# Interleaving the last products of one head group with the first products of the next

## The chip, the cores and the metric

The kernel runs on one core of one Trainium2 chip. The metric is the device time of one execution in microseconds (us). Before the change three executions took 440.07, 439.33 and 438.74 us; the median is 439.33 us.

## The reference

For each of 8 batches b there are 112 queries with 320 channels and a context of 375 tokens with 512 channels; the last 4 tokens are prompt tokens, the other 371 are text. There are 20 heads of 16 channels. What is computed, cut to its core:

```
q   = heads(x @ W_q);  k_t, v_t = heads(text @ W_k), heads(text @ W_v)
probs_t  = softmax(q @ k_t^T * scale)                  # 112 x 371 for each head
text_out = probs_t @ v_t
qsem     = probs_t @ text;  qsem /= |qsem|             # 512 channels for each head
fused    = q @ k_ip^T * scale + 0.5 * qsem @ ip_n^T    # 4 prompt tokens
ip_out   = (softmax(fused) * spatial_mask) @ v_ip
out      = (text_out + ip_out) @ W_out + b_out + x
```

Only the norm of qsem and its products with the 4 normalised prompt tokens are needed. With the Gram matrix G = text @ text^T, the squared norm is p^T G p. So the kernel multiplies the probabilities p of a head with G, the prompt products, a column of ones and the values v at once.

## The kernel before

**Groups.** The 20 heads of a batch are cut into 5 groups of 4 heads (`steps` lists all (b, g), 40 of them). A group is the unit of work around the change. Its four heads a = 0 to 3 use the four groups of 32 rows of TensorE's array; head a lies on partitions 32a to 32a+31.

**Products.** `multiplied` is the main part. The 371 text tokens are 12 blocks of 32. For block j = 0 to 11 and for each head a, one matmul takes the transposed probabilities of the block (32 rows, 112 queries) as weights and streams the block's part of a tile `u` past them: columns 32j to 392, of which the last 21 are prompt products, ones and values. G is symmetric, so only its upper part is used: block 0 streams 392 columns, block 1 360, and so on down to 72 columns for block 10 and 40 for block 11. The sums of a head gather in one PSUM bank. In the profile each float32 matmul appears as two passes, each with its own weight load (LDWEIGHTS, engine PEld), so 48 products are 96 MATMUL records.

**What follows.** ScalarE (ACT) copies the last 21 columns of each bank to `pvs` (`value_sums`, L705). VectorE (DVE) multiplies the first 371 columns with p and sums them (`reduced`, L738; a second instruction reads the accumulator). Both read the same bank, and the second reader waits for the first; `value_sums` stands first, so DVE waits for ACT. A bank is free again when both are done.

**Coming scores.** While a group is multiplied, the scores of the group two steps ahead are computed: one matmul of 375 columns for each head (`scores`, L632), the maximum on DVE (L645), the exponential on ACT (L649), a DMA from SP that spreads p over the ring `xg` (`probabilities`). A later DVE transposition makes the weights from it (`transposed`, L672).

**Pairs.** From the second group on, groups run in pairs without other TensorE work between them; there are 17 pairs, and 34 groups in them. Between the pairs stands full-array work of 7 to 11 us (projections, Gram matrices, and pieces of `finish`, here `f`, which ends a batch), written out in `behind`. One group before the first pair and the five of the last batch stand alone. The order on the engines around the change is the order of the code: TensorE, DVE, ACT, POOL and SP are scheduled by hand.

**PSUM banks.** There are 8: four of pool `ps_qd` ("qd"), two "sc" and two "mm". The first group of a pair multiplies into qd, and its coming scores use sc and mm. The second group multiplies into sc and mm, and its coming scores use qd: the scores of heads 2 and 3 stand after block 2 and take the first two qd banks of the first group, those of heads 0 and 1 stand after block 4 and take the other two. `turn` lists the banks that the work between pairs takes.

**POOL.** `placed` (L599) copies the next group's values into the last columns of `u` when the products that read the old ones are done.

Of the kernel before, what the change touches and what calls it, by code (L numbers as in the profile page):

```python
# [8 lines left out]
F32 = mybir.dt.float32  # L9
# [11 lines left out]
def kernel(  # L21
# [14 lines left out]
    nc = tc.nc  # L36
    P = 128
    B, S, C = x.shape
# [12 lines left out]
    RG = 32  # L51
# [625 lines left out]
    def multiplied(b, g, second=False):  # L677
        s = st[b]
        xT = s.pop(("xT", g))
        banks = []  # L680
        for a in range(GROUP):

            if b == B - 1 and g % 2 and g < NG - 1:
                banks.append(bank(f"ps_qd_{b}_{g}_{a}", spare=a > 1))
            elif second:
                banks.append(bank(f"ps_qd_{b}_{g}_{a}", spare=a < 2))
            else:
                banks.append(ps_qd.tile([P, 512], F32, tag="qd", name=f"ps_qd_{b}_{g}_{a}"))
        for j in range(BLK):
            c, q = j // QN, j % QN  # L690
            for a in range(GROUP):
                nc.tensor.matmul(  # L692
                    banks[a][:S, j * RG : UW],
                    xT[a * RG : (a + 1) * RG, j, :S],
                    region(b, c)[a * RG : (a + 1) * RG, q, q * RG :],
                    start=(j == 0),
                    stop=(j == BLK - 1),
                )
            yield
        s["qd", g] = banks  # L700
# [391 lines left out]
    def stretch(n, second):  # L1092

        b, g = steps[n]
        coming = steps[n + LEAD]
        late = None if second or not n else steps[n + 1]
        tags = ("mm", "sc") if b % 2 and g == NG - 1 else ("sc", "mm")
        places = {2: (2, "qd"), 4: (0, "qd")} if second else {0: (2, tags[0]), 1: (0, tags[1])}
        for j, _ in enumerate(multiplied(b, g, second)):
            if j in places:  # L1100
                a0, tag = places[j]
                for a in (a0, a0 + 1):
                    ps = pools[tag].tile([P, 512], F32, tag=tag, name=f"ps_s_{n + LEAD}_{a}")
                    scores(*coming, a, ps=ps)
                for a in (a0, a0 + 1):
                    probabilities(*coming, a)
                if late and a0 == 0:
                    transposed(*late, BLK // 2, BLK)
            if n and not second and j % QN == QN - 1:
                placed(*steps[n + 1], (j // QN,))  # L1110
# [16 lines left out]
    def behind(n):  # L1127
# [9 lines left out]
        if b % 2 == 0 and g == 0:  # L1137
# [18 lines left out]
            if n:  # L1156
                f(b - 1, 3)
# [14 lines left out]
        elif b % 2 == 0:  # L1172
            new = nb < B - 1
            turn[:] = ["qd"] * (2 + 2 * (b > 0) + (b == 0) + (not new)) + ["qd", "mm", "mm"] * new
# [34 lines left out]
        else:  # L1209
# [6 lines left out]
            f(b - 1)  # L1216
            tr(1)
            f(b - 1)
# [3 lines left out]
    for n, (b, g) in enumerate(steps[:-NG]):  # L1222
        second = n > 0 and n % 2 == 0
# [7 lines left out]
        moved(b, g)  # L1231
        if n and not second:
            if g > 1:
                turned(b + 2)
            if b % 2 and g in (0, NG - 1):
                f(b - 1 - (g == 0))
            continue
        if second and steps[n - 1] in ((b, 2), (b, 3)):
            turned(b + 2)
# [140 lines left out]
```

## Time and profile before

| what | value |
|---|---|
| median of three runs | 439.33 us |
| profiled execution, its own time | 439.46 us |
| span of its trace | 437.7 us |
| PE busy | 428.5 us, 98% |
| PEld busy (weight loads) | 330.9 us, 76% |
| DVE, ACT, POOL busy | 327.2, 185.9, 111.9 us |
| granted TensorE clock | 1.0 throughout |

PE stands for TensorE's matmuls, PEld for its weight loads, SP for the engine that issues most DMAs. A matmul record runs from its issue to a modelled end, and matmuls overlap, so a busy PE can still be late: what counts is when the next one starts. "32*112 32x360" is a weight of 32 rows and 112 columns, and 360 streamed columns.

### The profile page before, as it was taken

The page shows a single profiled execution, that of the slowest core. Times are in us where ns is not written, and L with a number is a line of the kernel's source. Part 1 is how long each engine was busy: PE and PEld are TensorE (multiplying, and loading weights), DVE is VectorE, ACT ScalarE, POOL GpSimd, SP SyncE. Part 2 cuts the span into 40 slices and gives each one's busy share as a digit, 9 for nine tenths or more (in the row PEclk, how much of TensorE's full clock was granted, in tenths as well). Part 3 has the DMA queues.
Part 4 walks back from the last instruction along what each step waited for, and adds up shares of the span by engine and source line. Part 5 has one row for each costly group of instructions (what it writes and reads, how often), then busy time and mean ns, then how long its engine had stood idle before and what let it go on. Part 6 is the DMA issues. An engine that isn't in the chain of part 4 may idle for free. (4 is left out here: it accounts for less than half of the span.)

```text
span 437.7 us, 12978 instructions
## 1 busy us (share of the span) xinstructions
PE 428.5 (98%) x5024; PEld 330.9 (76%) x5024; DVE 327.2 (75%) x687; ACT 185.9 (42%) x649; POOL 111.9 (26%) x270
## 2 busy tenths in 40 slices
PE   8999999999999999999999999999999999999986
PEld 8856776878686896878686887778776987777883
DVE  4045486877898887786798887796888897667884
ACT  2264132414543453424543363233632463336793
POOL 4302200021061242012160234002142226026440
PEclk9999999999999999999999999999999999999999
DMA  7569955577554656576654566475755426663300
GB/s 247 154 170 254 222 128 140 143 175 169 153 137 120 179 129 151 149 169 152 153 148 111 159 137 171 140 180 129 179 151 132 127 84 173 170 150 95 102 8 26
DMA packets 57931, 64.21 MB, mean 147 GB/s; under 512 B 18368, under 2 KB 52024, under 8 KB 57870
## 3 DMA queue, kind: packets, MB, share of 16 engines
q1 hardware_dynamic: 57304, 62.66, 56.6%
q8 instruction: 40, 0.66, 0.7%
q10 hardware_dynamic: 566, 0.72, 0.5%
q14 instruction: 21, 0.17, 0.1%
HBM read 18.67 MB, written 5.32 MB: 55 GB/s over the span
## 5 line engine op out<-in xcount | busy, mean ns | idle before, releaser
L692 PE MATMUL ps_qd<-u,xgT 32*112 32x168 f32 (+11 forms) x3840 | 221.3, 355 | 1.6 <-POOL u L599 1.6
L692 PEld LDWEIGHTS ps_qd<-u,xgT 32*112 32x112 f32 x3840 | 183.4, 171 | 33.3 <-issue 7.2
L672 DVE STREAM_TRANSPOSE xgT<-xg 128x768 f32<-128x768 f32 (+1 forms) x63 | 121.2, 1949 | 11.1 <-DMA xg<-p 11.1
L649 ACT ACTIVATE p<-ps_s,nmx 112x371 f32<-112x371 f32 x160 | 84.9, 592 | 93.9 <-DVE nmx L645 86.3
L738 DVE CUSTOM_DVE_ANT_0 junk<-ps_qd,p 112x371 f32<-112x371 f32 x148 | 80.2, 542 | 33.8 <-ACT pvs L705 18.2
L645 DVE TENSOR_REDUCE nmx<-ps_s 112x1 f32<-112x371 f32 x160 | 75.9, 535 | 22.3 <-PE ps_s L632 22.2
L599 POOL COPY u<-vr 128x64 f32<-128x64 f32 x120 | 26.7, 237 | 202.1 <-PE ps_qd L692 128.0
L632 PE MATMUL ps_s<-kT,qm 32*112 32x375 f32 (+1 forms) x320 | 68.3, 483 | 1.0 <-ACT shared L723 0.7
L526 PE MATMUL ps_v<-wv_sb,ctxT 128*128 128x384 f32 (+1 forms) x192 | 63.5, 477 | 0.3 <-ACT kT L499 0.3
L526 PEld LDWEIGHTS ps_v<-wv_sb,ctxT 128*128 128x128 f32 x192 | 35.4, 190 | 20.7 <-ACT kT L499 1.2
L492 PE MATMUL ps_k<-ctxT,wk_sb 128*128 128x371 f32 x136 | 45.8, 481 | 0.0
L632 PEld LDWEIGHTS ps_s<-kT,qm 32*112 32x112 f32 x320 | 35.0, 171 | 8.7 <-ACT shared L723 1.3
L454 PE MATMUL ps_g<-ctxT 128*128 128x375 f32 (+2 forms) x168 | 36.9, 376 | 0.1
L454 PEld LDWEIGHTS ps_g<-ctxT 128*128 128x128 f32 x168 | 28.2, 191 | 9.1 <-POOL ctxT L373 0.7
L492 PEld LDWEIGHTS ps_k<-ctxT,wk_sb 128*128 128x128 f32 x136 | 24.6, 190 | 13.4 <-issue 0.5
L533 ACT COPY vext<-ps_v 128x384 f32<-128x384 f32 (+1 forms) x24 | 11.2, 465 | 39.9 <-PE ps_v L526 39.9
L651 ACT COPY ipl<-ps_s 112x4 f32<-112x4 f32 x140 | 25.2, 180 | 0.0
L705 ACT COPY pvs<-ps_qd 112x21 f32<-112x21 f32 x150 | 16.4, 186 | 18.6 <-PE ps_qd L692 18.4
L336 DVE TENSOR_SCALAR qm<-ps_q,emask 128x224 f32<-128x224 f32 (+1 forms) x25 | 8.9, 394 | 19.7 <-PE ps_q L327 19.7
L499 ACT COPY kT<-ps_k 128x371 f32<-128x371 f32 x17 | 8.0, 469 | 34.6 <-PE ps_k L492 34.6
L443 ACT ACTIVATE ug<-ps_g 128x375 f32<-128x375 f32 (+2 forms) x24 | 9.0, 376 | 31.9 <-PE ps_g L454 21.0
L444 POOL TENSOR_TENSOR ug<-ug,half 128x128 f32<-128x128 f32 (+1 forms) x24 | 10.7, 447 | 39.4 <-ACT ug L443 39.4
(160 smaller groups left out, 332.4 us busy)
## 6 DMA issues: line engine op xcount, KB each, us to landing
xg<-p SPq DMA_DIRECT2D x159, 162.3 KB
u<-ug SPq DMA_DIRECT2D x128, 99.0 KB
ct<-in_ctx_dram SPq DMA_DIRECT2D x24, 176.0 KB
vr<-vd SPq DMA_DIRECT2D x32, 120.0 KB
vip<-vipd SPq DMA_DIRECT2D x6, 560.0 KB
vd<-vext SPq DMA_DIRECT2D x4, 480.0 KB
out_dram<-ob SPq DMA_DIRECT2D x8, 140.0 KB
ct<-in_ctx_dram SPq DMA_DIRECT2D x4, 256.0 KB
```

The lines of the kernel that those rows point to most:

```text
L454: nc.tensor.matmul(ps[:, : T - t0], ctxT[:, e, t0 : t0 + P], ctxT[:, e, t0:T], start=(e == 0), stop=(e == NE - 1),)
L492: nc.tensor.matmul(ps[:, :TT], wk_sb[:, e, i * P : (i + 1) * P], s["ctxT"][:, e, :TT], start=(e == 0), stop=(e == NE - 1),)
L526: nc.tensor.matmul(ps[:, :w], ctxT[:, e, c * P : (c + 1) * P], wv_sb[:, e, :w], start=(e == 0), stop=(e == NE - 1),)
L599: nc.gpsimd.tensor_copy(region(b, c)[:, :, UV - c * P :], s["vr"][:, c * QN : (c + 1) * QN, g, :])
L632: nc.tensor.matmul(ps[:S, :w], qm[a * RG : (a + 1) * RG, i, r, j * S : (j + 1) * S], s["kT"][a * RG : (a + 1) * RG, i, :w], start=True, st ...
L645: nc.vector.tensor_reduce(nmx, ps[:S, :TT], AX.X, ALU.max, negate=True)
L649: nc.scalar.activation(p, ps[:S, :TT], AF.Exp, bias=nmx)
L651: nc.scalar.copy(s["ipl"][:, groups[g][a], :], ps[:S, TT:T])
L672: nc.vector.transpose(xT[:, j : j + n].rearrange("p j (k q) -> p q j k", q=QN), xg[:, :, j * RG : (j + n) * RG].rearrange("p q (j k) -> p ...
L692: nc.tensor.matmul(banks[a][:S, j * RG : UW], xT[a * RG : (a + 1) * RG, j, :S], region(b, c)[a * RG : (a + 1) * RG, q, q * RG :], start=(j ...
L705: nc.scalar.copy(s["pvs"][:, h, :], ps[:S, TT:UW])
L738: nc.vector.tensor_tensor_reduce(out=junk, in0=ps[:S, :TT], in1=s["p", g][:, a, :], scale=1.0, scalar=0.0, op0=ALU.mult, op1=ALU.add, accu ...
```

## The change

Three things change inside a pair; its matmuls stay the same in number and size.

First, the last two blocks (72 and 40 columns) of the first group are no longer multiplied ahead of block 0 (392 columns) of the second group. Heads 2 and 3 do the second group's block 0 while heads 0 and 1 do the first group's last two blocks, and then the other way round. At the end of the second group, heads 2 and 3 do their last two blocks ahead of heads 0 and 1.

Second, the coming scores of the second group stand after blocks 4 and 7, where they stood after blocks 2 and 4.

Third, `reduced` of the first group stands ahead of its `value_sums`, so ACT now waits for DVE on each of these banks. Of the second group the order is as before.

With these the bank lists change a little: the second group's heads 2 and 3 now take the banks that heads 0 and 1 had, and in one stage the last projection takes an mm bank. Pieces of `finish` move to other places of the same stages.

TensorE, first pair of batch 1 (groups 0 and 1), where the groups meet. The tile `ps_qd_1_0_2` is the bank of batch 1, group 0, head 2; the last number is the matmul's streamed width. Before:

```order
L692 MATMUL ps_qd_1_0_0_1124<-u_1_408,xgT_1_0_1081 112x72
L692 MATMUL ps_qd_1_0_1_1125<-u_1_408,xgT_1_0_1081 112x72
L692 MATMUL ps_qd_1_0_2_1126<-u_1_408,xgT_1_0_1081 112x72
L692 MATMUL ps_qd_1_0_3_1127<-u_1_408,xgT_1_0_1081 112x72
L692 MATMUL ps_qd_1_0_0_1124<-u_1_408,xgT_1_0_1081 112x40
L692 MATMUL ps_qd_1_0_1_1125<-u_1_408,xgT_1_0_1081 112x40
L692 MATMUL ps_qd_1_0_2_1126<-u_1_408,xgT_1_0_1081 112x40
L692 MATMUL ps_qd_1_0_3_1127<-u_1_408,xgT_1_0_1081 112x40
L692 MATMUL ps_qd_1_1_0_1225<-u_1_408,xgT_1_1_1104 112x392
L692 MATMUL ps_qd_1_1_1_1226<-u_1_408,xgT_1_1_1104 112x392
L692 MATMUL ps_qd_1_1_2_1227<-u_1_408,xgT_1_1_1104 112x392
L692 MATMUL ps_qd_1_1_3_1228<-u_1_408,xgT_1_1_1104 112x392
```

The same place after:

```order
L683 MATMUL ps_qd_1_1_2_1202<-u_1_408,xgT_1_1_1104 112x392
L683 MATMUL ps_qd_1_1_3_1203<-u_1_408,xgT_1_1_1104 112x392
L683 MATMUL ps_qd_1_0_0_1124<-u_1_408,xgT_1_0_1081 112x72
L683 MATMUL ps_qd_1_0_1_1125<-u_1_408,xgT_1_0_1081 112x72
L683 MATMUL ps_qd_1_0_0_1124<-u_1_408,xgT_1_0_1081 112x40
L683 MATMUL ps_qd_1_0_1_1125<-u_1_408,xgT_1_0_1081 112x40
L683 MATMUL ps_qd_1_1_0_1200<-u_1_408,xgT_1_1_1104 112x392
L683 MATMUL ps_qd_1_1_1_1201<-u_1_408,xgT_1_1_1104 112x392
L683 MATMUL ps_qd_1_0_2_1126<-u_1_408,xgT_1_0_1081 112x72
L683 MATMUL ps_qd_1_0_3_1127<-u_1_408,xgT_1_0_1081 112x72
L683 MATMUL ps_qd_1_0_2_1126<-u_1_408,xgT_1_0_1081 112x40
L683 MATMUL ps_qd_1_0_3_1127<-u_1_408,xgT_1_0_1081 112x40
```

The twelve products are the same; two heads' long ones now stand ahead of the short ones.

TensorE, second group of the same pair, around the coming scores of heads 0 and 1 (`ps_s_8_0`, `ps_s_8_1`). Before:

```order
L692 MATMUL ps_qd_1_1_2_1227<-u_1_408,xgT_1_1_1104 112x264
L692 MATMUL ps_qd_1_1_3_1228<-u_1_408,xgT_1_1_1104 112x264
L632 MATMUL ps_s_8_0_1264<-kT_1_406,qm_1_811 112x375
L632 MATMUL ps_s_8_1_1266<-kT_1_406,qm_1_811 112x375
L692 MATMUL ps_qd_1_1_0_1225<-u_1_408,xgT_1_1_1104 112x232
```

After:

```order
L683 MATMUL ps_qd_1_1_2_1202<-u_1_408,xgT_1_1_1104 112x168
L683 MATMUL ps_qd_1_1_3_1203<-u_1_408,xgT_1_1_1104 112x168
L632 MATMUL ps_s_8_0_1276<-kT_1_406,qm_1_811 112x375
L632 MATMUL ps_s_8_1_1278<-kT_1_406,qm_1_811 112x375
L683 MATMUL ps_qd_1_1_0_1200<-u_1_408,xgT_1_1_1104 112x136
```

They moved from behind the 264-column products to behind the 168-column ones.

DVE, then ACT, the sums and value copies of the first group of that pair, with the engines that each waits for. Before:

```order
L738 ISA junk_1_0_1217,ss_1_411<-ps_qd_1_0_0_1124,p_1_0_864 112x371 [waits Activation_49]
L738 ISA ss_1_411 112x1
L738 ISA junk_1_2_1219,ss_1_411<-ps_qd_1_0_1_1125,p_1_0_864 112x371 [waits DVE_49,Activation_49]
...
L705 COPY pvs_1_412<-ps_qd_1_0_0_1124 112x21 [waits PE_49]
L705 COPY pvs_1_412<-ps_qd_1_0_1_1125 112x21 [waits PE_49]
```

After:

```order
L743 ISA junk_1_0_1221,ss_1_411<-ps_qd_1_0_0_1124,p_1_0_864 112x371 [waits PE_49]
L743 ISA ss_1_411 112x1
L743 ISA junk_1_2_1223,ss_1_411<-ps_qd_1_0_1_1125,p_1_0_864 112x371 [waits DVE_49,PE_49]
...
L710 COPY pvs_1_412<-ps_qd_1_0_0_1124 112x21 [waits DVE_49]
L710 COPY pvs_1_412<-ps_qd_1_0_1_1125 112x21 [waits DVE_49]
```

The wait has changed sides: the sums wait for TensorE alone, and each copy for its bank's sum.

The diff, cut to its core:

```diff
-    def multiplied(b, g, second=False):
+    def product(b, g, j, heads):
         s = st[b]
-        xT = s.pop(("xT", g))
...
+        xT = s["xT", g]
+        banks = s["qd", g]
+        c, q = j // QN, j % QN
+        for a in heads:
+            nc.tensor.matmul(
+                banks[a][:S, j * RG : UW],
+                xT[a * RG : (a + 1) * RG, j, :S],
+                region(b, c)[a * RG : (a + 1) * RG, q, q * RG :],
+                start=(j == 0),
+                stop=(j == BLK - 1),
+            )
...
-    def stretch(n, second):
-
-        b, g = steps[n]
-        coming = steps[n + LEAD]
-        late = None if second or not n else steps[n + 1]
+    def pair(n):
+
+        one, two = steps[n], steps[n + 1]
+        b, g = one
         tags = ("mm", "sc") if b % 2 and g == NG - 1 else ("sc", "mm")
-        places = {2: (2, "qd"), 4: (0, "qd")} if second else {0: (2, tags[0]), 1: (0, tags[1])}
...
+        ends = (BLK - 2, BLK - 1)
+
+        products_in(b, g, ("qd",) * GROUP)
+        for j in range(BLK - 2):
+            product(b, g, j, range(GROUP))
+            if j < 2:
+                heads = (HIGH, LOW)[j]
+                coming_scores(n + LEAD, heads, tags[j])
+                coming_probabilities(n + LEAD, heads)
+            if j == 1:
+                transposed(*two, BLK // 2, BLK)
+            if j % QN == QN - 1:
+                placed(*two, (j // QN,))
+        products_in(*two, (tags[1],) * 2 + (tags[0],) * 2)
+        for there, here in ((HIGH, LOW), (LOW, HIGH)):
+            product(*two, 0, there)
+            for j in ends:
+                product(b, g, j, here)
+        del st[b]["xT", g]
+        placed(*two, (NT - 1,))
+        moved(b, g)
+        if g > 1:
+            turned(b + 2)
+        if b % 2 and g in (0, NG - 1):
+            f(b - 1 - (g == 0))
+        if g in (1, 2):
+            f(b - 1, 3 - g)
+        reduced(b, g)
+        value_sums(b, g)
+
+        b, g = two
+        for j in range(1, BLK - 2):
+            product(b, g, j, range(GROUP))
+            if j == 4:
+                coming_scores(n + 1 + LEAD, HIGH, "qd")
+                coming_probabilities(n + 1 + LEAD, HIGH)
+            if j == 7:
+                coming_scores(n + 1 + LEAD, LOW, "qd")
+                coming_probabilities(n + 1 + LEAD, LOW)
+        for heads in (HIGH, LOW):
+            for j in ends:
+                product(b, g, j, heads)
...
-            turn[:] = ["qd"] * (2 + 2 * (b > 0) + (b == 0) + (not new)) + ["qd", "mm", "mm"] * new
+            turn[:] = ["qd"] * (3 + (b > 0)) + (["qd", "mm", "mm"] if new else ["mm"])
...
-        if second:
-            f1 = steps[n - 1]
-            if f1[1] == 1 or f1[1] == 2:
-                f(f1[0] - 1)
-            value_sums(*f1)
-            reduced(*f1)
-        stretch(n, second)
...
+    for n in range(0, len(steps) - NG, 2):
+        if n:
+            pair(n - 1)
+        else:
+            alone(n)
```

HIGH is heads 2 and 3, LOW heads 0 and 1; NT is 3, QN 4, BLK 12.

More of the change, by code (lines that the diff above doesn't have):

```diff
@@ L675, in transposed, with products_in, multiplied @@
             )
[L677 removed]
+    def product(b, g, j, heads):
         s = st[b]
[L679 to L698 removed]
+        xT = s["xT", g]
[9 more added lines that the diff above has]
+            )
+    def products_in(b, g, tags):
+        st[b]["qd", g] = [
+            pools[tag].tile([P, 512], F32, tag=tag, name=f"ps_qd_{b}_{g}_{a}")
+            for a, tag in enumerate(tags)
+        ]
+    def multiplied(b, g):
+        turned_round = b == B - 1 and g % 2 and g < NG - 1
+        products_in(b, g, ("mm", "mm", "sc", "sc") if turned_round else ("qd",) * GROUP)
+        for j in range(BLK):
+            product(b, g, j, range(GROUP))
             yield
[L700 removed]
+        del st[b]["xT", g]
     def value_sums(b, g, a0=0):
@@ L1090, in turned @@
             run(("c", b), lambda: transposed_context(b), pieces)
-    def stretch(n, second):
-        b, g = steps[n]
-        coming = steps[n + LEAD]
-        late = None if second or not n else steps[n + 1]
-        tags = ("mm", "sc") if b % 2 and g == NG - 1 else ("sc", "mm")
-        places = {2: (2, "qd"), 4: (0, "qd")} if second else {0: (2, tags[0]), 1: (0, tags[1])}
[L1099 to L1110, printed above, removed]
+    LOW, HIGH = (0, 1), (2, 3)
```

38 lines of the change are left out of this document (24 added, 14 removed).

## The prediction

> **What bounds the kernel now.** I read the page first: what is busy, and which lines carry it.
>
> ```profile
> span 437.7 us, 12978 instructions
> PE 428.5 (98%) x5024; PEld 330.9 (76%) x5024; DVE 327.2 (75%) x687; ACT 185.9 (42%) x649; POOL 111.9 (26%) x270
> ...
> L692 PE MATMUL ps_qd<-u,xgT 32*112 32x168 f32 (+11 forms) x3840 | 221.3, 355 | 1.6 <-POOL u L599 1.6
> ...
> L738 DVE CUSTOM_DVE_ANT_0 junk<-ps_qd,p 112x371 f32<-112x371 f32 x148 | 80.2, 542 | 33.8 <-ACT pvs L705 18.2
> ```
>
> TensorE sets the end: it is busy for 98%, and the products (L692) are half of that. DVE waited 18.2 us for ACT's value copies ahead of its sums (last row). But matmul records overlap, so a row of the array that starts its next product late leaves no idle time. So I cut the trace by stages. The 17 pairs of groups, the last batch's first group and the sum over these 18 stretches, from the view by windows (columns: length, then busy time and count of PE, PEld, DVE, ACT, POOL):
>
> ```profile
> core 0: us, PE busy (x) PEld busy (x) DVE busy (x) ACT busy (x) POOL busy (x), PEclk, DMA share, GB/s
> 55.44:66.37 10.93, 10.93 (x210) 9.13 (x209) 8.76 (x18) 4.80 (x14) 1.19 (x5) 1.00 0.46 115
> ...
> 97.08:108.02 10.94, 10.94 (x209) 9.12 (x208) 7.42 (x17) 5.02 (x22) 2.78 (x9) 1.00 0.71 155
> ...
> 217.57:229.02 11.45, 11.45 (x209) 9.17 (x208) 9.73 (x22) 5.39 (x23) 6.02 (x7) 1.00 0.47 128
> ...
> 355.44:366.83 11.39, 11.39 (x209) 9.99 (x208) 9.16 (x26) 5.88 (x25) 5.97 (x7) 1.00 0.37 96
> 375.32:386.26 10.94, 10.94 (x209) 9.14 (x208) 7.43 (x17) 5.17 (x22) 0.71 (x3) 1.00 0.65 177
> 392.20:398.81 6.61, 6.13 (x105) 5.30 (x104) 5.27 (x7) 3.92 (x16) 1.24 (x4) 1.00 0.31 86
> sum 194.50, PE 194.02 PEld 166.93 DVE 153.84 ACT 92.21 POOL 53.94; mean PE 10.78 PEld 9.27 DVE 8.55 ACT 5.12 POOL 3.00
> ```
>
> The pairs take 194.50 - 6.61 = 187.9 us, 11.05 us each; the clock is 1.00. Now the pair at 97.08 (batch 1, groups 0 and 1) in its halves, and the group that stands alone at 36.74, all three with the same 48 products and four scores:
>
> ```profile
> 97.08:102.33 5.25, 5.25 (x105) 1.00 0.40 123
> 102.33:108.02 5.69, 5.69 (x115) 1.00 0.98 185
> 36.74:42.10 5.36, 5.36 (x104) 1.00 0.91 255
> ```
>
> The second half takes 0.33 us more than a lone group, which even begins on an empty array. A pair of a first half and a lone group would take 5.25 + 5.36 = 10.6 us, so 0.45 us of the mean pair is something else. The timeline of that second half shows what (PEld, PE, DVE, each in its own order):
>
> ```profile
> 104.94 0.17 PEld L632 LDWEIGHTS ps_s<-kT,qm 32*112 32x112 f32 x1
> ...
> 105.44 0.17 PEld L632 LDWEIGHTS ps_s<-kT,qm 32*112 32x112 f32 x1
> ...
> 105.16 0.47 PE L632 MATMUL ps_s<-kT,qm 32*112 32x375 f32 x1
> 105.36 0.39 PE L692 MATMUL ps_qd<-u,xgT 32*112 32x264 f32 x2
> ...
> 102.75 0.55 DVE L738 CUSTOM_DVE_ANT_0 junk<-ps_qd,p 112x371 f32<-112x371 f32 x1 [0.66 <-ACT pvs L705]
> ...
> 104.14 0.54 DVE L738 CUSTOM_DVE_ANT_0 junk<-ps_qd,p 112x371 f32<-112x371 f32 x1
> ...
> 104.83 0.54 DVE L738 CUSTOM_DVE_ANT_0 junk<-ps_qd,p 112x371 f32<-112x371 f32 x1
> 105.30 0.08 DVE L738 DVE_READ_ACCUMULATOR2_ANT ss<- 112x1 f32 x1
> ```
>
> The scores of heads 0 and 1 take the first group's last two banks. Head 0's weights load at 104.94. Head 1's load only at 105.44, just after DVE has read the fourth sum (105.30 + 0.08 = 105.38). Head 1's row of the array was free when head 0's was, at 105.16; it streams from about 105.54, one load later (0.10 us, below). It is 0.38 us late, has no slack left before the pair's end, and TensorE counts it as busy. So each pair ends on the chain value copies, four sums of 0.69 us each, last score.
>
> **Part 1: the last short products among the long ones.** The place where the groups meet, by windows: blocks 8 to 11 of the first group (136, 104, 72, 40 columns), then blocks 0 and 1 of the second (392, 360), and from the timeline the weight loads there:
>
> ```profile
> 101.58:101.81 0.23, 0.23 (x16) 0.23 (x12) 0.23 (x1) 0.00 (x0) 0.00 (x0) 1.00 1.22 331
> 101.81:102.00 0.19, 0.19 (x16) 0.19 (x12) 0.19 (x1) 0.00 (x0) 0.08 (x1) 1.00 0.66 164
> 102.00:102.17 0.17, 0.17 (x16) 0.17 (x13) 0.09 (x1) 0.00 (x0) 0.16 (x1) 1.00 1.15 331
> 102.17:102.33 0.16, 0.16 (x18) 0.16 (x16) 0.00 (x0) 0.00 (x0) 0.00 (x0) 1.00 0.71 199
> 102.33:103.06 0.73, 0.73 (x19) 0.46 (x16) 0.31 (x1) 0.41 (x4) 0.24 (x1) 1.00 1.00 208
> 103.06:103.67 0.60, 0.60 (x12) 0.38 (x8) 0.46 (x3) 0.00 (x0) 0.00 (x0) 1.00 0.95 145
> ...
> 101.44 1.81 PEld L692 LDWEIGHTS ps_qd<-u,xgT 32*112 32x112 f32 x48
> ```
>
> 360 columns take 0.605 us, 1.68 ns a column. At that rate 104, 72 and 40 columns would take 0.175, 0.12 and 0.07 us; they take 0.19, 0.17 and 0.16, and the 392-column block behind them 0.73 in place of 0.66. So 0.23 us is lost for each meeting: two weight loads for each short block need about 0.2 us, 0.10 each. What are the loads bound by? The last row has 48 loads within 1.81 us, at 171 ns each: 8.2 us of loading, so the four rows load at once. Each row is bound by its own loads. Its sequence of two short blocks and one long block takes 4 x 0.10 + 0.66 us in either order, so I take a gain of 0. The bounds for a pair: -0.23 us, if a row's loads go faster while other rows stream, and +0.39, if a row may not run ahead of the others (rivals).
>
> The Trainium skill ("TensorE: Matmul & The Clock Gate", Part 3, "The mechanism") says that a weight load overlaps running matmuls only when they are in another row group. By that the change would hide all four short loads behind the other rows' long block, and the sum would be the first rival's. Here the trace disagrees: the 360-column block keeps to its streaming time, 0.60 us, with its own rows' loads within it.
>
> At the end of the second group, heads 2 and 3 now do their last blocks ahead of 0 and 1, which are fed about one load later: +0.10 us a pair, or 17 x 0.10 = +1.7 us (0 to +0.39 a pair).
>
> **Parts 2 and 3: later scores, sums first.** On the same pair's clock: the second group's block 0 can start when the 104-column block is done, 102.00. Heads 0 and 1 finish the first group's bank at 102.00 + 0.39 = 102.4, heads 2 and 3 at 102.00 + 0.66 + 0.39 = 103.05, where all rows are level again. A finished bank is read 0.2 us later (block end 102.33, first copy at 102.53):
>
> ```profile
> 102.53 0.41 ACT L705 COPY pvs<-ps_qd 112x21 f32<-112x21 f32 x4 [1.03 <-PE ps_qd L692]
> ```
>
> So the sums run from 102.6 to 102.9 on, as now from 102.75, since they no longer wait for copies. With 0.69 us each, the second is read by 104.3 and the fourth by 105.4 to 105.7. A copy behind each (0.19 us, and about 0.1 to start) frees the banks at 104.6 and 105.7 to 106.0. Scores after block 4 are due at 103.05 + (360+328+296+264) x 1.68 ns = 105.15, after block 7 at 103.05 + 1848 x 1.68 ns = 106.15, their loads 0.14 us ahead of that. Both find their banks free, by 0.4 us and by 0.0 to 0.3 us. So the 0.45 us goes: 17 x 0.45 = -7.6 us (at least the 0.33 seen against the lone group, 5.6 us).
>
> In some pairs DVE turns a context slice ahead of the sums. From the view by groups, from that of the waits, and from the timeline for part 4:
>
> ```profile
> L385 DVE STREAM_TRANSPOSE ctxT<-ct 128x512 f32<-128x512 f32 x18 | 19.2, 1067 | 0.0
> ...
> DVE xgT L672 <- DMA xg<-p: 1.1, 1, 1.1
> ...
> 392.92 0.17 PEld L692 LDWEIGHTS ps_qd<-u,xgT 32*112 32x112 f32 x1 [0.44 <-DVE ob L868]
> ```
>
> There the sums end later. In the four slowest pairs (11.11 to 11.45 us) I leave 0.2 us of waiting: +0.8 us (0 to 0.45 each). What is late next: ACT's four copies wait on DVE with the next exponentials behind them, but those need scores that are due later still. The second group's scores reach ACT 0.6 to 0.9 us later, and so SP's four DMAs of p, the DMAs queued behind them, and DVE's transposition. That one waits now for at most 1.1 us in one stage (second row), at the end of 7 to 11 us of full-array work, for a group that is multiplied 5 us later. I cost this at nothing; without that cover it would be up to 0.9 us in a pair.
>
> POOL's last third of the values is placed about 0.7 us later than now against the second group's start; the products that read it (block 8) come 3.5 us after. Nothing.
>
> **Part 4: the last batch's first group.** It takes 6.61 us against 5.36 alone. Its fourth head starts at 392.92, 0.72 us behind the stage, since its bank is held by the projection that DVE still adds up (ob, third row). That projection now has an mm bank, and the fourth head waits for something older. I take -0.5 us (0 to -0.72; part of it may return as another wait).
>
> **Sum.** -7.6 + 1.7 + 0.8 - 0.5 = -5.6 us. The profiled execution took 439.46 us, 0.13 over the median of 439.33, so the prediction is 433.9 us. A change under 0.3% (1.3 us) could not be told from none.
>
> **Rivals.**
>
> *The interleave hides the loads too.* Then 17 x 0.23 = 3.9 us more: 430.0. Against it: the 48 loads in 1.81 us, which leave no shared path that could be relieved.
>
> *The rows are held to the order of the program.* Then heads 2 and 3 cannot start their short blocks until heads 0 and 1 have begun the second pass of theirs: 0.39 us for a meeting, and 0.39 rather than 0.10 at the pair's end. With the waits gone a pair costs 0.78 - 0.45 = +0.33 us: 17 x 0.33 - 0.5 = +5.1, or 444.6 us, slower. It decides from 0.45 us of lost lead in a pair. Against it stands the PE pair of rows above: head 0's score starts at 105.16, the 264-column products of heads 2 and 3 at 105.36, though these stand ahead of it in the program. But that is a lead of two instructions; the change needs more.
>
> The same page, "What overlaps and what doesn't", has matmuls start and end strictly in program order, which is this rival; the two rows just named disagree with it.
>
> *The wait comes back as a copy.* If the sums start only when all four rows have finished, and a signal is late by another 0.3 us, the fourth copy ends at 106.5, the score is 0.4 us late again, and only part 4 remains: about 439 us, no change. The slack of 0.0 to 0.3 us speaks for it, that the sums need no copies first against it.
>
> **How the numbers follow.** The forecast (waits go, loads gain nothing) has 0.66, with a range of its own of 432 to 436 from the bounds of its terms. Loads hidden too: 0.10. Rows held in order: 0.10. The wait back as a copy: 0.09. The remaining 0.05 is for something slower that I do not see. The range from 430.0 to 437.5 holds the forecast, the first rival and a part of the third. Faster: 0.66 + 0.10 and 0.03 of the third rival, 0.79. Same: 0.06 of the third and 0.02 of the second, 0.08. Slower: the rest, 0.13.
>
> **What would show it.** Pairs of 10.6 to 10.8 us; the two score loads of heads 0 and 1 some 0.01 us apart rather than 0.50; sums that no longer wait for ACT in a pair's first group. At the meeting, 0.39 us for the short blocks of one half beside the other half's 392 columns. I am wrong if the LOW scores still load apart, if a row stands still at a meeting, or if the work between pairs grows.

## The result and the profile after

The changed kernel takes 434.4 us (median of six executions, 433.69 to 435.09), the kernel before 439.96 us (median of six, 438.74 to 440.39). The ratio is 0.9877, with a 95% interval from 0.9861 to 0.9894: 5.6 us faster.

The page of the changed kernel; of the groups the products, the sums and the value copies:

```profile
span 432.9 us, 12985 instructions
PE 423.2 (98%) x5024; PEld 323.8 (75%) x5024; DVE 328.5 (76%) x687; ACT 190.7 (44%) x649; POOL 112.1 (26%) x270
...
L683 PE MATMUL ps_qd<-u,xgT 32*112 32x232 f32 (+11 forms) x3840 | 215.4, 352 | 1.9 <-POOL u L599 1.9
...
L743 DVE CUSTOM_DVE_ANT_0 junk<-ps_qd,p 112x371 f32<-112x371 f32 x148 | 80.2, 542 | 31.5 <-ACT pvs L710 11.4
...
L710 ACT COPY pvs<-ps_qd 112x21 f32<-112x21 f32 x150 | 21.4, 200 | 62.2 <-DVE ss L743 61.0
```

The wait has changed sides: DVE waits 11.4 us for ACT instead of 18.2 (what is left belongs to the second groups and to groups that stand alone), and ACT now waits 61.0 us for DVE. PE is busy 5.3 us less. The pairs by windows (length first, as in the prediction), five of the 17 and the sum of all:

```profile
56.65:67.33 10.68, 10.68 (x210) 8.82 (x209) 7.26 (x17) 4.26 (x12) 1.19 (x5) 1.00 0.41 105
...
154.08:164.94 10.86, 10.86 (x210) 10.81 (x209) 9.53 (x26) 5.01 (x20) 5.39 (x9) 1.00 0.53 127
...
216.28:226.98 10.70, 10.70 (x210) 8.86 (x209) 9.19 (x23) 4.77 (x19) 4.68 (x5) 1.00 0.49 135
...
351.52:362.80 11.28, 11.28 (x209) 10.53 (x208) 9.96 (x26) 5.26 (x21) 5.70 (x8) 1.00 0.37 96
371.29:381.99 10.70, 10.70 (x209) 8.85 (x209) 7.27 (x18) 4.54 (x18) 0.71 (x3) 1.00 0.68 184
sum 182.79, PE 182.79 PEld 156.02 DVE 147.38 ACT 77.70 POOL 47.78; mean PE 10.75 PEld 9.18 DVE 8.67 ACT 4.57 POOL 2.81
```

The pairs fell from 187.9 to 182.8 us. Fourteen of them take 10.68 to 10.71 us. Three, those of groups 1 and 2 of batches 2, 4 and 6, take 10.86, 10.86 (at 253.01) and 11.28; I name a pair by the batch and number of its first group and call them the pairs (even b, 1).

Three more stages differ. By windows, first of the kernel before the stage with the prompt projections and the one behind batch 0 group 4, then of the changed kernel the same two and the last batch's first group:

```profile
42.10:55.44 13.34, 13.11 (x68) 8.99 (x64) 5.94 (x13) 2.51 (x11) 2.62 (x9) 1.00 1.07 239
87.22:97.08 9.86, 9.76 (x45) 7.17 (x44) 8.75 (x16) 1.99 (x9) 1.44 (x6) 1.00 0.86 198
```

```profile
41.62:56.65 15.03, 14.80 (x69) 9.45 (x65) 7.27 (x13) 2.52 (x11) 2.62 (x9) 0.89 1.04 217
87.83:97.33 9.50, 9.50 (x46) 7.25 (x45) 9.07 (x15) 2.94 (x12) 1.50 (x6) 1.00 0.85 197
387.93:393.98 6.05, 5.43 (x106) 4.27 (x105) 5.13 (x8) 3.80 (x16) 1.03 (x4) 1.00 0.29 80
```

The span fell by 4.8 us: pairs -5.1, the last batch's first group -0.56 (6.61 before), the stage behind batch 0 group 4 -0.36, the time ahead of 42 us -0.48, and +1.69 in the stage with the prompt projections. I count neither of the last two for the change. The stage with the prompt projections had a granted clock of 0.89 in this execution and of 1.00 in that of before (last section). It begins anywhere from 41.1 to 42.4 us in the profiled executions of the changed kernel and of its variants below, which are alike up to there. So 6.0 us of the trace are left for the change. The other stages are the same to 0.02 us.

Now the place the prediction is about, the second group of the pair at 97.33 (batch 1, groups 0 and 1), by the timelines of PEld, DVE and ACT:

```profile
105.20 0.18 PEld L632 LDWEIGHTS ps_s<-kT,qm 32*112 32x112 f32 x2
...
106.45 0.27 PEld L632 LDWEIGHTS ps_s<-kT,qm 32*112 32x112 f32 x4
...
103.19 0.54 DVE L743 CUSTOM_DVE_ANT_0 junk<-ps_qd,p 112x371 f32<-112x371 f32 x1 [0.88 <-PE ps_qd L683]
...
105.75 0.08 DVE L743 DVE_READ_ACCUMULATOR2_ANT ss<- 112x1 f32 x1
...
104.47 0.18 ACT L710 COPY pvs<-ps_qd 112x21 f32<-112x21 f32 x1 [0.52 <-DVE ss L743]
...
105.86 0.18 ACT L710 COPY pvs<-ps_qd 112x21 f32<-112x21 f32 x1 [0.52 <-DVE ss L743]
```

The scores of heads 2 and 3 load at 105.20, when the second bank has been free since 104.47 + 0.18 = 104.65. Those of heads 0 and 1, both passes of both, load within 0.27 us at 106.45, where before the two heads stood 0.50 us apart. The fourth bank is free at 105.86 + 0.18 = 106.04, 0.4 us earlier. No score waits for a bank in this pair.

### The profile page after: what moved, and what is told of

It reads as the page before. It is cut to its first block, busy times and chain, and to the rows that moved or that the text cites. A ratio compares the mean times of both kernels' runs of the same rounds, so it can differ in the third digit from the quotient of the medians.

```text
span 432.9 us, 12985 instructions
## 1 busy us (share of the span) xinstructions
PE 423.2 (98%) x5024; PEld 323.8 (75%) x5024; DVE 328.5 (76%) x687; ACT 190.7 (44%) x649; POOL 112.1 (26%) x270
## 5 line engine op out<-in xcount | busy, mean ns | idle before, releaser
L683 PE MATMUL ps_qd<-u,xgT 32*112 32x232 f32 (+11 forms) x3840 | 215.4, 352 | 1.9 <-POOL u L599 1.9
L683 PEld LDWEIGHTS ps_qd<-u,xgT 32*112 32x112 f32 x3840 | 180.0, 172 | 36.5 <-issue 8.1
L649 ACT ACTIVATE p<-ps_s,nmx 112x371 f32<-112x371 f32 x160 | 85.8, 586 | 52.5 <-DVE nmx L645 48.5
L743 DVE CUSTOM_DVE_ANT_0 junk<-ps_qd,p 112x371 f32<-112x371 f32 x148 | 80.2, 542 | 31.5 <-ACT pvs L710 11.4
L645 DVE TENSOR_REDUCE nmx<-ps_s 112x1 f32<-112x371 f32 x160 | 77.3, 537 | 28.0 <-PE ps_s L632 26.0
L632 PE MATMUL ps_s<-kT,qm 32*112 32x375 f32 (+1 forms) x320 | 61.9, 487 | 1.0 <-ACT shared L728 0.7
L710 ACT COPY pvs<-ps_qd 112x21 f32<-112x21 f32 x150 | 21.4, 200 | 62.2 <-DVE ss L743 61.0
L632 PEld LDWEIGHTS ps_s<-kT,qm 32*112 32x112 f32 x320 | 27.9, 171 | 6.9 <-ACT shared L728 1.3
L651 ACT COPY ipl<-ps_s 112x4 f32<-112x4 f32 x140 | 24.2, 173 | 0.0
```

The lines of the kernel that those rows point to most:

```text
L632: nc.tensor.matmul(ps[:S, :w], qm[a * RG : (a + 1) * RG, i, r, j * S : (j + 1) * S], s["kT"][a * RG : (a + 1) * RG, i, :w], start=True, st ...
L645: nc.vector.tensor_reduce(nmx, ps[:S, :TT], AX.X, ALU.max, negate=True)
L649: nc.scalar.activation(p, ps[:S, :TT], AF.Exp, bias=nmx)
L651: nc.scalar.copy(s["ipl"][:, groups[g][a], :], ps[:S, TT:T])
L683: nc.tensor.matmul(banks[a][:S, j * RG : UW], xT[a * RG : (a + 1) * RG, j, :S], region(b, c)[a * RG : (a + 1) * RG, q, q * RG :], start=(j ...
L710: nc.scalar.copy(s["pvs"][:, h, :], ps[:S, TT:UW])
```

## Experiments

Ratios are to runs of the kernel before on the same chip. Those scatter by about 1% (beside the first set of runs from 439.2 us at a granted clock of 1.00 to 444.6 us at 0.988), so the sum of the 17 pairs in the trace is the sharper measure. It is 187.9 us before and 182.8 after. By small moves I mean what came with the three parts of the change: pieces of `finish` and the transposition of a context slice that stand in other places, and the mm bank for one projection.

### One part of the change alone

**Later scores alone** (the kernel before, one line):

```
-        places = {2: (2, "qd"), 4: (0, "qd")} if second else {0: (2, tags[0]), 1: (0, tags[1])}
+        places = {4: (2, "qd"), 7: (0, "qd")} if second else {0: (2, tags[0]), 1: (0, tags[1])}
```

> The kernel before with one edit: the second group's coming scores stand after blocks 4 and 7 rather than 2 and 4; no interleave, copies still ahead of sums. Theory (each pair loses its time in the last scores' wait for banks): the wait goes here too, the pairs shrink from 11.05 us to the 10.70 us that the changed kernel shows, 17 x 0.35 = 6.0 us less than before, about 434 us. Rival (the interleave brings the gain by hiding weight loads): no gain, about 440 us.

Measured: 437.78 us, ratio 0.9908 (0.9873 to 0.9942). Windows of two of its pairs, the sum of all 17, and the two other stages:

```profile
98.50:109.20 10.70, 10.70 (x209) 8.66 (x208) 7.26 (x17) 4.08 (x18) 2.77 (x9) 1.00 0.66 144
...
353.83:365.65 11.82, 11.82 (x209) 10.77 (x208) 10.07 (x26) 4.86 (x21) 6.89 (x9) 1.00 0.32 84
...
sum 184.39, PE 184.39 PEld 157.17 DVE 145.50 ACT 72.32 POOL 53.22; mean PE 10.85 PEld 9.25 DVE 8.56 ACT 4.25 POOL 3.13
```

```profile
88.03:98.50 10.47, 9.76 (x46) 7.17 (x44) 9.65 (x17) 2.94 (x12) 1.50 (x6) 1.00 0.86 191
390.78:397.40 6.62, 6.14 (x106) 5.31 (x105) 5.46 (x8) 3.93 (x16) 1.60 (x4) 1.00 0.34 93
```

Fourteen pairs are already as short as in the changed kernel. So the two numbers that say where the scores stand carry the pairs' gain, copies first and all. But three pairs (11.40, 11.38, 11.82) and two other stages are 3.1 us longer than there: 1.6 + 0.97 + 0.57.

**Sums ahead of copies alone** (the kernel before):

```
-            value_sums(*f1)
             reduced(*f1)
+            value_sums(*f1)
```

> The kernel before, with the sums of a pair's first group put ahead of its value copies and nothing else (the coming scores still stand after blocks 2 and 4). Theory (the banks come free too late for early scores whichever reader goes first): a last reader ends one sum chain after the bank is full either way; the copy behind the last sum adds up to 0.2 us where it took none, so the pairs stay at 11.0 to 11.3 us and the kernel within -0.5 to +4 us of the kernel before. Rival (the wait of the sums for the copies is what cost the 0.45 us): the sums start 0.2 us earlier, the last score with them, pairs of about 10.8 us, -3 us or more.

Measured: ratio 1.0031 (0.9997 to 1.0065).

```profile
sum 189.67, PE 189.67 PEld 162.27 DVE 148.21 ACT 94.62 POOL 53.33; mean PE 11.16 PEld 9.55 DVE 8.72 ACT 5.57 POOL 3.14
```

The pairs get 1.8 us longer in sum. Where a context slice keeps DVE busy ahead of the sums, the copy that now ends behind the last sum adds 0.2 us (the pair at 76.18 from 11.04 to 11.23); in others the length stays at 10.94. The stage behind batch 0 group 4 takes 9.50 us here too, so its 0.36 us come with this edit as well.

**The interleave alone**, with the bank lists and the small moves that belong to it (the changed kernel, with the other two parts taken back):

```
-        reduced(b, g)
         value_sums(b, g)
+        reduced(b, g)
...
-            if j == 4:
+            if j == 2:
...
-            if j == 7:
+            if j == 4:
```

> The changed kernel with the other two parts taken back: second group's scores after blocks 2 and 4, value copies ahead of the sums. What stays of the change is the interleave (with the second group's banks that go with it) and the small moves, which alone were worth nothing. Theory (the interleave puts the last two heads' short blocks behind a 392-column block, so their banks are full 0.66 us later, and early scores wait for just those banks): pairs of 11.3 to 11.6 us, 4 to 9 us slower than the kernel before. Rival (the interleave brings the gain and the later scores only follow it): faster than the kernel before by 3 us or more.

Measured: ratio 1.0093 (1.0060 to 1.0127), 0.9% slower. By windows, and from the timeline of DVE:

```profile
98.39:109.74 11.35, 11.35 (x210) 9.56 (x209) 7.41 (x17) 5.13 (x21) 2.77 (x9) 1.00 0.65 150
...
sum 194.36, PE 194.36 PEld 166.87 DVE 150.57 ACT 90.27 POOL 51.00; mean PE 11.43 PEld 9.82 DVE 8.86 ACT 5.31 POOL 3.00
```

```profile
104.45 0.55 DVE L743 CUSTOM_DVE_ANT_0 junk<-ps_qd,p 112x371 f32<-112x371 f32 x1 [1.08 <-ACT pvs L710]
```

The first sum starts 6.06 us into the pair, against 102.75 - 97.08 = 5.67 before: 0.39 us later. The same pair is 0.41 us longer (11.35 against 10.94, and 10.94 also with the small moves alone, below). The interleave delays the banks, and scores that already wait for them pay all of it.

**The small moves alone** (the kernel before):

```
-                f(f1[0] - 1)
+                f(f1[0] - 1, 3 - f1[1])
...
-            turned(b + 2)
+            turned(b + 2, 1 + (steps[n - 1] == (0, 3)))
...
-                f(b - 1, 3)
+                f(b - 1, 2)
...
-            turn[:] = ["qd"] * (2 + 2 * (b > 0) + (b == 0) + (not new)) + ["qd", "mm", "mm"] * new
+            turn[:] = ["qd"] * (3 + (b > 0)) + (["qd", "mm", "mm"] if new else ["mm"])
...
+            f(b - 1, 2)
             tr(1)
-            f(b - 1)
```

(In the last piece, one step of finish goes from behind `tr(1)` to ahead of it.)

> The kernel before with the three small moves alone (piece of finish, both context slices, mm bank); scores after blocks 2 and 4, copies first, no interleave. Theory: only the stage behind batch 0 group 4 (9.87 to about 9.5 us) and batch 7 group 0 (6.62 to about 6.05) get shorter, the pairs stay at 11.05 us on the mean, since their wait is not touched: -0.9 us, no more than can be told from no change. Rival (the moves are worth the 3 us by themselves): -2.5 us or more.

Measured: ratio 1.0029 (0.9993 to 1.0066).

```profile
135.42:146.80 11.38, 11.38 (x210) 9.39 (x209) 9.94 (x20) 4.76 (x20) 1.27 (x6) 1.00 0.39 103
...
sum 188.96, PE 188.96 PEld 161.03 DVE 150.97 ACT 88.60 POOL 52.70; mean PE 11.12 PEld 9.47 DVE 8.88 ACT 5.21 POOL 3.10
```

The two stages get shorter as expected (9.49 and 6.05 us), but three pairs, of group 4 of an odd batch and group 0 of the next, get 0.35 us longer each, so nothing is gained. That half was missed by both theories. In the pair shown a transposition has moved in, and DVE starts the first sum 141.52 - 135.42 = 6.10 us into it, against 141.31 - 135.55 = 5.76 before. The early scores pay that, too.

### Later scores with the small moves

Both edits together on the kernel before: later scores and small moves, without interleave, copies first, banks in the old order.

> The run with later scores alone, plus the small moves of the change: one piece of finish (its last sum and weights on DVE) from the stage ahead of the pair (even b, 1) to behind the maxima and the transposition inside it; both context slices turned ahead of the sums of batch 0 group 4; an mm bank for the last projection ahead of batch 7. No interleave, copies first, old order of the second group's banks. Theory (these three moves are the 3 us by which the run with later scores alone stays behind the changed kernel): the three pairs of 11.38 to 11.82 us come to 10.9, 10.9 and 11.3, the stage behind batch 0 group 4 from 10.48 to 9.50 us, batch 7 group 0 from 6.62 to 6.05: the changed kernel's time within 0.3%, about 3.2 us below the run with later scores alone. Rival (the order of the second group's banks matters too): the pairs or the stage stay longer and 1 us or more of the 3 is left.

Measured: 435.02 us, ratio 0.9865 (0.9822 to 0.9908).

```profile
sum 182.79, PE 182.79 PEld 153.17 DVE 146.93 ACT 72.70 POOL 51.78; mean PE 10.75 PEld 9.01 DVE 8.64 ACT 4.28 POOL 3.05
```

Pairs, stages (9.49, 6.05 us) and span (432.9 us) are those of the changed kernel. So the gain is there without two of the three parts, and the order of the second group's banks shows no gain either. What the small moves do is seen in the run with later scores alone. In its stage at 88.03 DVE turns the second context slice only behind the four sums, POOL adds its last columns to it, and TensorE waits for those (row of that run's PE timeline below). In its pairs (even b, 1) a last sum of finish, waiting for ACT, stands ahead of the maxima.

```profile
93.23 5.34 PE L454 MATMUL ps_g<-ctxT 128*128 128x375 f32 x24 [0.71 <-POOL ctxT L373]
```

### The change less one part

**Without the interleave** (the changed kernel; the end of the second group is put back in the same way):

```
-        for there, here in ((HIGH, LOW), (LOW, HIGH)):
-            product(*two, 0, there)
-            for j in ends:
-                product(b, g, j, here)
+        for j in ends:
+            product(b, g, j, range(GROUP))
+        product(*two, 0, range(GROUP))
```

> The changed kernel with both interleavings undone: all four heads finish the first group's last two blocks ahead of the second group's block 0, and the last blocks of the second group go side by side. Theory (loads are bound within a row, so the interleave is worth nothing): 434.4 us as changed, or down to 432.7 if the pair's end costs the 0.10 us that was charged to it. Rival (loads hidden by the other rows' long products, 0.23 us a pair): 17 x 0.23 = 3.9 us slower, 438.3 us.

Measured: 434.8 us, ratio 0.9838 (0.9794 to 0.9882). By windows a pair in its halves, the sum of all pairs, and from the timeline of DVE the first sum:

```profile
96.33:101.58 5.25, 5.25 (x107) 4.20 (x108) 3.97 (x8) 2.47 (x9) 2.05 (x6) 1.00 0.48 123
101.58:107.03 5.45, 5.45 (x115) 4.47 (x109) 3.86 (x12) 1.92 (x9) 0.71 (x3) 1.00 0.96 179
...
sum 182.80, PE 182.80 PEld 152.93 DVE 148.31 ACT 77.68 POOL 51.70; mean PE 10.75 PEld 9.00 DVE 8.72 ACT 4.57 POOL 3.04
```

```profile
101.78 0.55 DVE L743 CUSTOM_DVE_ANT_0 junk<-ps_qd,p 112x371 f32<-112x371 f32 x1 [0.47 <-PE ps_qd L683]
```

The interleave is worth nothing, to 0.01 us over 17 pairs. Outside the pairs one stage of this execution, behind the pair at 272.67, took 12.06 us, against 10.81 to 10.88 in the twelve others: TensorE waited 0.98 us for POOL, whose copies had waited for a DMA. Whether the edit had a part in that is not shown. The interleave is not without effect, though: the first sum starts 101.78 - 96.33 = 5.45 us into the pair, with the interleave 103.19 - 97.33 = 5.86. Those 0.41 us are hidden in the changed kernel only because the scores stand late.

**With the copies first again** (the changed kernel, `value_sums` ahead of `reduced` in the pair):

> The changed kernel with the first group's value copies ahead of its sums again. Theory (the later scores have 0.0 to 0.3 us in hand, the order of the two readers shifts a bank's release by about 0.1 us): same as changed, 434.4 us within 1 us. Rival (sums ahead of copies carry the gain): the wait is back in each pair, 438 to 440 us.

Measured: 435.22 us, ratio 0.9841 (0.9797 to 0.9885).

```profile
sum 182.78, PE 182.78 PEld 155.97 DVE 147.59 ACT 74.32 POOL 47.75; mean PE 10.75 PEld 9.17 DVE 8.68 ACT 4.37 POOL 2.81
```

The order of the two readers is worth nothing either.

**With the early scores again** (the changed kernel, 2 and 4 in place of 4 and 7):

> The changed kernel with the second group's coming scores after blocks 2 and 4 as before the change; interleave and sums-first stay. Theory: the first group's banks now come free later (104.6 and 105.7 to 106.0 on the prediction's clock), the scores are due at 104.2 and 105.15; the last waits 0.55 to 0.85 us, a pair takes 11.2 to 11.5 us, and the kernel 434.4 + 17 x (0.5 to 0.8) = 443 to 448 us, slower than the kernel before. Rival (interleave brings the gain): 434.4 us.

Measured: 446.92 us, ratio 1.0122 (1.0070 to 1.0174).

```profile
sum 194.89, PE 194.89 PEld 166.87 DVE 152.94 ACT 94.42 POOL 50.92; mean PE 11.46 PEld 9.82 DVE 9.00 ACT 5.55 POOL 3.00
```

With the early scores, the rest of the change is a loss of 7 us in the pairs.

### How much slack, and what holds the last three pairs

**Scores of heads 0 and 1 after block 6** (the changed kernel):

```
-            if j == 7:
+            if j == 6:
```

> The changed kernel with the scores of heads 0 and 1 after block 6 instead of block 7, the interleave and all else as in the change. Theory (the second two banks come free about when the scores after block 7 are due): due 0.34 us earlier they wait in the pairs, 0.1 to 0.3 us in each, 2 to 5 us slower than the changed kernel, if the rows have no lead left to spend. Rival (the banks are free well before, and what holds the scores after block 7 is the feeding of rows that run out of step): no slower than the changed kernel, pairs of 10.6 to 10.7 us.

Measured: 435.82 us, ratio 0.9894 (0.9845 to 0.9942). Two pairs and the sum:

```profile
96.77:107.45 10.68, 10.68 (x209) 8.81 (x208) 7.81 (x20) 4.35 (x18) 2.76 (x9) 1.00 0.66 145
...
134.64:145.48 10.84, 10.84 (x209) 9.01 (x208) 10.01 (x20) 4.24 (x17) 1.26 (x6) 1.00 0.45 117
...
sum 183.40, PE 183.40 PEld 156.63 DVE 150.47 ACT 78.80 POOL 47.15; mean PE 10.79 PEld 9.21 DVE 8.85 ACT 4.64 POOL 2.77
```

The theory fell for most pairs: they are 0.02 us shorter, not 0.1 to 0.3 longer. It holds for four (134.64, 215.78, 233.93, 332.93), by 0.14 to 0.31 us. In the first of these DVE comes to the sums 6.09 us into the pair, behind a context slice (timeline below), where it is 5.86 in the pair of the result section. In sum block 7 is the better place, and in those four pairs block 6 uses up the slack.

```profile
140.73 0.53 DVE L743 CUSTOM_DVE_ANT_0 junk<-ps_qd,p 112x371 f32<-112x371 f32 x1
```

**The last sum of finish behind the sums** (the changed kernel):

```
-        if g in (1, 2):
-            f(b - 1, 3 - g)
+        if g == 2:
+            f(b - 1)
         reduced(b, g)
         value_sums(b, g)
+        if g == 1:
+            f(b - 1, 2)
```

> The changed kernel, with the last sum and the weights of finish on DVE (0.95 us, lines 822 to 826) behind the four sums of the pair (even b, 1) instead of ahead of them. Theory (in these pairs the scores after block 7 wait for sums that stand behind 0.95 us of other DVE work): the pairs of 10.86, 10.86 and 11.28 us lose what the sums cause, 0.16 us each, so 10.7, 10.7 and 11.1, the rest of the third being its late first product (0.3 us behind an ACT copy): 0.3 to 0.5 us less in the trace, not to be told in the time. Rival (the copies or the feeding hold these scores): the three pairs keep their lengths, or the 0.95 us comes back in the next maxima and makes them longer.

Measured: 434.16 us, ratio 0.9836 (0.9803 to 0.9869).

```profile
153.18:164.04 10.86, 10.86 (x210) 10.81 (x209) 9.37 (x26) 4.63 (x18) 2.66 (x7) 1.00 0.53 126
...
sum 182.79, PE 182.79 PEld 156.01 DVE 148.51 ACT 76.55 POOL 39.50; mean PE 10.75 PEld 9.18 DVE 8.74 ACT 4.50 POOL 2.32
```

My theory fell: the three pairs keep their lengths, though 0.95 us of other work no longer stand ahead of the sums. What is left is their first product. In the changed kernel ACT copies the last piece of the Gram matrix out of a qd bank only behind two table loads of 1.28 us each (the second load and the copy are the first two rows, from the timeline of ACT), and in the pair at 351.52 a head's first weights wait for that copy (timeline of PEld):

```profile
152.64 1.28 ACT L802 ACT_TABLE_LOAD   x1
153.93 0.27 ACT L443 ACTIVATE ug<-ps_g 128x119 f32<-128x119 f32 x1
...
352.12 0.17 PEld L683 LDWEIGHTS ps_qd<-u,xgT 32*112 32x112 f32 x1 [0.32 <-ACT ug L443]
```

**The Gram copy first** (the changed kernel):

```
         nc.scalar.activation(rn, rn, AF.Sqrt)
-        nc.scalar.preload_act_table(AF.Exp)
+        if b % 2 == 0:
+            nc.scalar.preload_act_table(AF.Exp)
...
         yield
+        if b % 2:
+            nc.scalar.preload_act_table(AF.Exp)
...
-            if n:
-                f(b - 1)
             gr(nb)
+            if n:
+                f(b - 1)
```

> The changed kernel with another order on ACT ahead of the pairs (even b, 1): the last copy of the Gram matrix (line 443) goes ahead of the square root of finish and its two table loads of 1.28 us each, and the second table load goes behind the copy of the values. Theory (in these three pairs one head starts 0.16, 0.16 and 0.60 us late, because ACT still holds its bank for that Gram copy behind the table loads, and the pair never gets it back): all three pairs at 10.7 us, the sum of the pairs 0.9 us shorter, 181.9 us; the time 0.2% below the changed kernel, too little to be told in the time but not in the trace. Rival (the table loads come back in another place): the exponential of finish, the scores of heads 0 and 1 or the stage ahead get longer, and the sum of stage and pair stays where it is.

Measured: 437.06 us, ratio 0.9883 (0.9835 to 0.9931).

```profile
154.11:164.81 10.70, 10.70 (x210) 8.84 (x209) 9.46 (x26) 6.14 (x20) 4.95 (x7) 1.00 0.54 128
...
351.23:362.01 10.78, 10.78 (x209) 8.92 (x209) 9.92 (x26) 6.16 (x20) 5.27 (x7) 1.00 0.36 94
...
sum 181.97, PE 181.97 PEld 150.67 DVE 147.13 ACT 80.75 POOL 46.27; mean PE 10.70 PEld 8.86 DVE 8.65 ACT 4.75 POOL 2.72
```

The late head was the cause: 0.16, 0.16 and 0.50 us come off, the stages ahead keep their lengths (8.14, 8.14, 7.71 us), and the span of this execution is 432.1 us against 432.9. It is the shortest sum of pairs of all. In the times it can't be told from the changed kernel.

## Why the prediction was right, step by step

The forecast was -5.6 us and 433.9 us; measured were -5.6 us and 434.4 us, from a median of the kernel before that is 0.5 us above the 439.46 us from which the prediction counted. That the two differences agree to a tenth is partly luck. In the trace 6.0 us are left for the change, and five of the six timed executions had a granted clock of 0.995, as had the profiled one, which lost 1.69 us in one stage. In the pairs, too, forecast and trace agree at -5.1 us, but there two errors of the sum cancel.

**What bounds the kernel: right.** Scores that wait for banks were most of the 0.45 us of a pair. Later scores alone take fourteen pairs from 11.04 us on the mean to 10.70, which is 0.34 us, and early scores in the changed kernel bring the wait back. No run moves the scores of heads 0 and 1 alone from their old place, so their share beside that of heads 2 and 3 is not shown.

**Parts 2 and 3 (-7.6 + 0.8): the cause right, the size 1.7 us too large, one half of the reason wrong.** The whole 5.1 us of the pairs are theirs, where 6.8 were forecast: the pairs stop at 10.70 us, not at the 10.6 us of a first half and a lone group. The prediction had the sums start from 102.6 to 102.9 on the clock of before, 5.5 to 5.8 us into the pair, because they need no copies. They start at 5.86, later than before (5.67): the interleave takes 0.41 us, which the prediction did not count (last section). Putting the sums first is worth nothing with late scores and costs 1.8 us of pairs with early ones, so the pairs' gain is the place of the scores alone. The last bank is free 8.71 us into the pair (106.04 - 97.33), inside the forecast 8.6 to 8.9. The slack of the scores after block 7 is 0.4 us, where 0.0 to 0.3 was forecast.

**The four slowest pairs (+0.8): right in sum, wrong in place.** Of the pairs of 11.45, 11.11, 11.19 and 11.39 us three came down to 10.70 or 10.71. The 0.9 us above 10.70 sit in the three pairs (even b, 1), and their cause is not DVE's sums but a head whose first product comes late, behind a Gram copy on ACT: with that copy moved, 0.8 of the 0.9 us are gone.

**Part 1 (0): right.** The meeting, from the end of the 136-column block to block 1 of the second group, takes 1.25 us with the interleave and without, in the changed kernel and in the one before:

```profile
102.06:103.31 1.25, 1.25 (x43) 1.15 (x37) 0.37 (x2) 0.00 (x0) 0.24 (x1) 1.00 0.92 213
```

```profile
101.81:103.06 1.25, 1.25 (x40) 0.98 (x36) 0.59 (x2) 0.41 (x4) 0.48 (x2) 1.00 0.93 217
```

**The pair's end (+1.7): wrong.** With the end put back in the old order the pairs keep their 10.70 us, so heads 2 and 3 first cost nothing. But the second half still takes 5.45 us (10.70 less a first half of 5.25), 0.09 more than the lone group's 5.36. The +0.10 us a pair hit this by chance, and that is why the sum of the pairs came out right. Where the 0.09 us sit isn't settled; scores one block earlier took 0.02 of them.

**Knock-on at nothing: true only with the small moves.** With them the later scores bring 5.10 + 0.56 + 0.36 = 6.0 us of trace; without them 3.1 us less. The prediction priced one of these moves (part 4, -0.5, measured -0.56) and missed that the later scores lose these 3.1 us, in three pairs and two stages, where the other moves are missing. It missed the -0.36 us in the stage behind batch 0 group 4, too.

**The rivals.** That the interleave hides the loads: no, it gains 0.00 us. The Trainium skill ("TensorE: Matmul & The Clock Gate", Part 3, "The mechanism") has a weight load overlap running matmuls only when they are in another row group. By that rule the change would be worth 3.9 us more (an estimate of the prediction, from its rows); the run without the interleave disagrees, 182.80 against 182.79 us. So do the first products of the pair at 97.33: all four rows start their first pass by 97.35, the weights of their second pass load from 97.42 on for 0.17 us, and that pass streams from 97.75. The prediction's own argument, that the 360-column block keeps to its streaming time, says less, since it had the rate of 1.68 ns a column from that block; but 0.23 us for 136 columns give the same rate. That rows are held to program order: no, there was no loss at the meeting. That the wait comes back as a copy: no, the fourth copy ended 0.4 us ahead of the score's load.

## What to carry to other kernels

When a stage waits for a buffer, look first whether the consumer can come later: here two numbers in a table did what two reorderings of the producers could not. Find out what an earlier reader or an interleave does to the moment at which the buffer is released, since a change that costs nothing in one place can lengthen that chain and be paid by whoever already waits for it. And when an edit moves work of other engines along with the main one, price each of these moves, because the gain can depend on them.

## What was not expected of the hardware

**Rows start out of program order, but their ends are told in it.** In the changed kernel heads 0 and 1 fill their banks behind a 104-column block and two short ones, by about 102.06 + 0.19 + 0.39 = 102.64. The first sum starts at 103.19. The 392-column products of heads 2 and 3, which stand ahead of the short ones in the program, are through at about 103.31 - 0.39 = 102.92. Without the interleave the first sum starts 5.45 us into the pair, 0.2 us behind its short blocks.

The packed trace also has the counter (semaphore) for which these sums wait; it rises once for each finished bank. In this pair it first rises at 103.165. That is 0.42 us behind the modelled end of the last product of head 0 (102.74), but 0.07 us behind the modelled end of the 392-column products of heads 2 and 3 (103.09). In all 17 pairs the first rise comes 0.06 to 0.08 us behind that end, also in the three where a head is late. In the run without the interleave, in the pair at 96.33, it first rises at 101.753, 0.01 us behind the modelled end of head 0's last product (101.74). The Trainium skill ("TensorE: Matmul & The Clock Gate", Part 3, "What overlaps and what doesn't") has matmuls start and end strictly in program order: the starts disagree, as the prediction showed, and the ends agree as far as the counter tells them. By these figures that order is the 0.41 us by which the interleave delays the sums.

**A clock that drops in the middle of a stage that counts as busy.** Eight small matmuls of the prompt projections, first in the changed kernel, then in the one before (windows; the granted clock stands third from the end):

```profile
49.88:53.80 3.92, 3.92 (x9) 1.25 (x8) 0.19 (x1) 0.19 (x1) 0.00 (x0) 0.56 1.13 199
```

```profile
50.36:52.60 2.24, 2.24 (x9) 0.80 (x8) 0.19 (x1) 0.18 (x1) 0.00 (x0) 1.00 1.06 193
```

The same work took 3.92 us at a clock of 0.56 and 2.24 us at 1.00. The stage took 15.0 us in eight of the thirteen profiled executions of all kernels and 13.3 us in the others, with no relation to their edits. A span of one execution must be cleared of these 1.7 us before it is compared.

**A late head was not caught up.** In the changed kernel a first product that came 0.16 us late made its pair 0.16 us longer at its end, ten microseconds later; with the head on time (the last experiment) the pair was back at 10.70 us. In the kernel before the same head was as late, but there its pair, at 154.70, took 10.97 us, no longer than most others, which waited for banks.
